# Keys ahead of queries, split projections stored in the layout of the tiles, and one product for the gates of all batches

## The chip, the cores and the metric

One core of a Trainium2 chip runs one program. The core has five engines with a queue of instructions each: TensorE (PE, matrix products; PEld is its loading of weights), VectorE (DVE), ScalarE (ACT), GpSimd (POOL) and SyncE (SP). SP issues most DMA transfers here, ACT and POOL a few. Each engine works through its queue in order and waits on semaphores where it needs another's result. The metric is the device time of one execution in microseconds. A time is the median of several runs; beside it there is one profiled execution, whose span and trace are quoted.

## The reference

A transformer block with adaptive layer norm, on 4 batches of 512 tokens of width 256, in float32:

```
mod = silu(c) @ wmod                      # six vectors of 256 for each batch: sa, ca, ga, sb, cb, gb
ga, gb: sign kept, magnitude at least 0.25
h = layernorm(x) * (1 + ca) + sa
x = x + ga * attention(h)                 # 32 heads of 8, 8 key/value heads, causal
h = layernorm(x) * (1 + cb) + sb
x = x + gb * ffn(h)                       # 16 experts of 176, 4 of them for each token,
                                          # and a shared expert of 352
```

The gate `ga` is needed where the attention is added to `x`, the vectors `sb`, `cb` and the gate `gb` only after that.

## The kernel before, in words

**Packs.** The attention is done in 16 packs, four for each batch. A pack has two key heads and their eight query heads. Queries and keys are split into three bfloat16 parts each (high, middle, low), so that one product of depth 72 (3 x 3 parts x 8) gives scores of float32 quality. For a pack, `qx` (a tile of 128 rows by 8 heads by 512 tokens) holds in its first 72 rows the query parts, and `kx` the key parts, arranged so that each pair of parts meets. There are three `qx` and three `kx`, used in turn by the packs.

**From projection to tile.** `norm1(b, due)` does a batch's first layer norm (`layernorm`: statistics, a power on POOL, four normalizations), two turns on PE with a modulating copy into `ht` on ACT, and then `split` for the queries of the first two packs, for the keys of all four packs, and for the queries of the last two; last `project_v` for the values. A `split` is a PE pass of two products, then on ACT and DVE in turn `high`, `rest`, `mid`, `low` into a tile `pt`, then stores from `pt` into small DRAM tensors on SP (line 762): `qd` (three parts by 64 rows by 512 tokens, 192 KB) and `kd` (48 KB) for each pack. `load(s)` (lines 815 to 822) reads them back into `qx` and `kx`: three transfers for the queries, each of 24 rows, and nine for the keys, each of 8 rows. For packs 0 and 1 ACT issues the key loads, for the others SP. Unused rows of `qx` and `kx` are filled once (`unused`, lines 512 and 513, on DVE; two of the three pairs wait for the first key store).

**Maxima, scores, weighing.** `row_max(s)` runs ahead of a pack: 22 units of PE products into two buffers `pr` (lines 860 and 868), each reduced to maxima on DVE (line 881). `shift(s)` splits the maxima in three parts (DVE), turns them (PE, line 920), copies them to `mrow` (ACT, line 930) and puts them as three more rows into `qx` with a transfer on SP (line 940, 24 KB). Only then can `pack(s)` compute scores (PE, line 1001), exponentials (ACT, 1013), the causal cut (POOL, 1020) and the weighing of values (PE, 971). `finish` copies the sum to `yr` (ACT, 1047), turns it and divides. After the fourth pack of a batch `after(b)` projects with `wo`, multiplies by the gate `g_sb` and adds to `x_sb`; `norm2(b)` does the second layer norm with `m2_sb`, the gating and the scattering of rows to the experts. The experts and the shared expert follow in `ffn`.

**Modulation.** `modulate_first` computes `sa` and `ca` for the first norm at the start. `modulation(b, last, due)` (lines 571 to 611), called for each batch in turn, computes the other four vectors: two PE passes of four products each (line 580), for which one batch's column of `sct` is repeated over 128 columns, so that the result stands in all 128 partitions. From the first pass `sign`, `size` and `gates` make the two gates (DVE, 128 x 512), from the second ACT copies the other two vectors into `m2_sb`.

**What sets the order.** The order on PE, DVE, ACT and SP is written out by a planner. `plan.add` takes an engine, an estimated cost, a function, the operations it needs, a due time (in packs), and what buffers (`hold`) it takes and gives. `plan.go` picks the operation that could start first by these costs, and among equals the one due first. The resulting order is fixed before the program runs; a wait that is longer than planned holds what is behind it on that engine. SP's transfers use eight semaphores in rotation, and a transfer waits until the one that had its semaphore before has landed.

**The start.** SP's order in the kernel before is: input loads with the first quarter of `x`; the stores and loads of packs 0 and 1; `later_loads` (line 1383: the other three quarters of `x`, and the weights of the gating, of the shared expert and of `wo`); the stores and loads of pack 2; `blank_all` (line 1394: 4.4 MB of zeros and one block of marked rows into DRAM); then the first `mrow` transfer. The calls of `modulation` wait for the loads of pack 1, and `norm1(1)` for `later_loads`.

## Time and profile before

| what | value |
|---|---|
| median of 3 runs | 754.57 us (753.82 to 755.66) |
| profiled execution: its time, its span | 746.31 us, 744.4 us |
| PE busy | 651.1 us (87%) |
| DVE busy | 455.6 us (61%) |
| share of the chain that ended last: PE, DVE, DMA | 66%, 17%, 6% |
| DMA packets | 54969, 74.51 MB |
| first product of the maxima, first of the scores | 31.0 us, 67.8 us |
| last `yr` copy of the attention | 421.9 us |

The profile page of one execution gives busy times of the engines, the span in 40 slices, the chain of work that ended last (followed back from the last instruction, at each step to what released it), the costliest groups of instructions, and the DMA issues. The trace can also be asked for the instructions of a stretch in order of time (start, duration, engine, source line, operation, output<-inputs; in brackets the idle time before it and what ended that), and for sums over stretches (busy time of each engine with its number of instructions, then the granted PE clock, the busy share of the 16 DMA engines, and what they moved). `SPq` and `ACTq` are transfers issued by SP and ACT: their duration is that of the issue, not of the transfer.

### The profile page before, as it was taken

How to read it: one execution, taken by the hardware profiler on the slowest of the kernel's cores; microseconds unless marked ns; L12 is line 12 of the kernel's file. 1: busy time of each engine (PE TensorE's matmuls, PEld its weight loads, DVE VectorE, ACT ScalarE, POOL GpSimd, SP SyncE). 2: the span in 40 equal slices, each digit the busy share in tenths (PEclk: the TensorE clock that was granted, in tenths of full speed). 3: DMA queues.
4: the chain of work that ended last, by engine and by line, in shares of the span. 5: the costliest groups of instructions: out<-in, count | busy, mean ns of one | idle time of the engine just before them, and what ended most of it. 6: DMA issues, size and time to landing. Idle time of an engine off the chain costs nothing.

```text
span 744.4 us, 12881 instructions
## 1 busy us (share of the span) xinstructions
PE 651.1 (87%) x4205; PEld 411.5 (55%) x4236; DVE 455.6 (61%) x1286; ACT 317.4 (43%) x557; POOL 346.2 (47%) x449
## 2 busy tenths in 40 slices
PE   5576999999999999999987897599999999999920
PEld 3343455555544554445443385488777777777710
DVE  4695868778888888787885056644333333333417
ACT  2103654575556654564655411022444444444400
POOL 4000222335257462673736643722566666556632
PEclk9787999999999999999999799799999999999965
DMA  4585211111133220332101196821576666666575
GB/s 135 128 253 198 72 27 41 42 42 47 29 100 102 65 64 13 108 102 57 42 11 55 63 300 200 205 69 30 96 110 110 109 110 110 102 108 110 66 188 186
DMA packets 54969, 74.51 MB, mean 100 GB/s; under 512 B 8024, under 2 KB 48056, under 8 KB 53752
## 3 DMA queue, kind: packets, MB, share of 16 engines
q1 hardware_dynamic: 37992, 51.99, 25.1%
q0 software_dynamic: 14448, 19.31, 16.0%
q10 hardware_dynamic: 2464, 2.39, 1.1%
q8 instruction: 35, 0.57, 0.3%
q14 instruction: 30, 0.25, 0.1%
HBM read 41.11 MB, written 32.16 MB: 98 GB/s over the span
## 4 chain that ended last, share of the span: by engine, by line
PE 66%; DVE 17%; DMA 6%; POOL 3%; issue 3%; ACT 2%; ACTq 0%; another core or an unknown queue 0%; SPq 0%; DVEq 0%; POOLq 0%
PE pu L1524 13%; PE py L1552 9%; PE pa L971 8%; PE pr L860 8%; PE p L1001 6%; DVE mx_s L881 6%; PE pu L416 5%; PE py L454 3%; PE pr L868 2%; PE pb L1543 2%; PE pt L1504 2%; DMA s<-acc_d 2%; PE p L580 1%; ACT ex L1013 1%; DMA kx<-kd 1%
## 5 line engine op out<-in xcount | busy, mean ns | idle before, releaser
L881 DVE TENSOR_REDUCE mx_s<-pr 128x1 f32<-128x384 f32 (+3 forms) x352 | 212.6, 635 | 52.6 <-PE pr L868 50.5
L1013 ACT ACTIVATE ex<-p 128x1024 f32<-128x1024 f32 (+1 forms) x192 | 163.2, 880 | 103.3 <-PE p L1001 77.4
L1020 POOL TENSOR_SCALAR_AFFINE_SELECT ex<-ex 128x256 f32<-128x256 f32 (+1 forms) x192 | 93.5, 493 | 180.2 <-ACT ex L1013 177.8
L1565 POOL DMA_INDIRECT acc_d<-y_b,token x79 | 123.0, 1556 | 77.2 <-DVE token L1514 32.3
L860 PE MATMUL pr<-kx,qx 125*128 125x384 bf16 (+3 forms) x512 | 125.2, 309 | 20.9 <-DVE mx_s L881 10.0
L1524 PE MATMUL pu<-up_sb,xt 128*128 x316 | 106.6, 460 | 0.0
L1001 PE MATMUL p<-qx,kx 128*128 128x384 bf16 (+3 forms) x481 | 92.0, 299 | 9.5 <-DMA qx<-mrow 6.5
L971 PE MATMUL pa<-ex,vaug 128*32 128x512 f32 (+3 forms) x1024 | 96.8, 450 | 2.5 <-POOL ex L1020 1.0
L860 PEld LDWEIGHTS <-qx 125*128 125x128 bf16 x512 | 47.0, 101 | 77.4 <-issue 49.7
L868 PE MATMUL pr<-seen,ident_h 128*128 128x128 bf16 (+2 forms) x352 | 88.5, 251 | 0.0
L1552 PE MATMUL py<-down_sb,at_b 88*128 x316 | 81.5, 379 | 1.2 <-DVE at_b L1547 1.2
L1342 POOL DMA_INDIRECT rows_d<-row,slot x64 | 64.2, 1003 | 25.7 <-DVE slot L1339 13.0
L1552 PEld LDWEIGHTS py<-down_sb,at_b 88*128 88x128 f32 x316 | 59.7, 189 | 21.9 <-ACT y_b L1562 1.7
L1538 DVE TENSOR_TENSOR a_b<-sg_b,pu 128x176 f32<-128x176 f32 x79 | 26.6, 337 | 71.7 <-ACT sg_b L1534 71.6
L1001 PEld LDWEIGHTS <-kx 128*128 128x128 bf16 x512 | 40.8, 98 | 40.9 <-issue 25.8
L1524 PEld LDWEIGHTS pu<-up_sb,xt 128*128 128x128 f32 x316 | 53.9, 190 | 16.7
L1562 ACT ACTIVATE y_b<-py,cw_b 128x256 f32<-128x256 f32 x79 | 37.4, 473 | 46.5 <-PE py L1552 46.5
L1547 DVE COPY at_b<-pb 88x256 f32<-88x256 f32 x79 | 33.2, 420 | 29.7 <-PE pb L1543 29.7
L1534 ACT ACTIVATE sg_b<-pu 128x176 f32<-128x176 f32 x79 | 25.1, 317 | 60.6 <-PE pu L1524 58.3
L416 PE MATMUL pu<-h2t,sup_sb 128*128 128x256 f32 (+1 forms) x192 | 48.2, 402 | 1.7 <-DVE a L436 1.7
L868 PEld LDWEIGHTS <-ident_h 128*128 128x128 bf16 x352 | 35.0, 99 | 22.8 <-issue 15.7
L416 PEld LDWEIGHTS pu<-h2t,sup_sb 128*128 128x128 f32 (+1 forms) x192 | 36.6, 193 | 9.8 <-DVE a L436 2.0
(176 smaller groups left out, 738.2 us busy)
## 6 DMA issues: line engine op xcount, KB each, us to landing
x<-rows_d SPq DMA_DIRECT2D x79, 136.5 KB
qx<-qd SPq DMA_DIRECT2D x48, 192.0 KB
up_sb<-in_up_t SPq DMA_DIRECT2D x8, 704.0 KB
acc_d<-blank SPq DMA_DIRECT2D x2, 2176.0 KB
qd<-pt SPq DMA_DIRECT2D x16, 192.0 KB
down_sb<-in_down_t SPq DMA_DIRECT2D x8, 352.0 KB
rows_d<-blank SPq DMA_DIRECT2D x17, 136.5 KB
x_sb<-in_x SPq DMA_DIRECT2D x4, 512.0 KB
```

The costliest lines, as they stand in the source:

```text
L416: nc.tensor.matmul(st["p"][:rows, w, :], lhsT=sup_sb[:, k, c0 : c0 + rows], rhs=h2t[:, k, c1 : c1 + half], start=(k == 0), stop=(k == KC - 1),
L860: nc.tensor.matmul(pr[:, h, :], lhsT=qx[s % 3][:QKZ, REP * j + r + h, ts(i, P)], rhs=kx[s % 3][:QKZ, j, :w], start=True, stop=False, skip_ ...
L868: nc.tensor.matmul(pr[:, :, w - P :], lhsT=ident_h, rhs=seen.unsqueeze(1).to_broadcast([P, n, P]), start=False, stop=True, skip_group_chec ...
L881: nc.vector.tensor_reduce(mx[s][:, i, c0 : c0 + n], st["pr"], AX.X, ALU.max)
L971: nc.tensor.matmul(st["pa"][32 * r : 32 * r + 32, c * P :], lhsT=vaugs[b % 2][:, c, SLOTS * n + j, :], rhs=exs[r], start=(j == 0 and c == ...
L1001: nc.tensor.matmul(pe[:, h, :], lhsT=kx[s % 3][:, j, ts(c, P)], rhs=qx[s % 3][:, REP * j + r + h, c * P :], start=True, stop=True,)
L1013: nc.scalar.activation(ex, st["pe"], AF.Exp, scale=qk_scale)
L1020: nc.gpsimd.affine_select(out=st["ex"][:, :, 0:P], in_=st["ex"][:, :, 0:P], pattern=[[0, n], [1, P]], base=0, channel_multiplier=-1, compa ...
L1342: dma = nc.gpsimd.indirect_dma_start(out=rows_d, out_offset=bass.IndirectOffsetOnAxis(ap=st["slot"][:, i, k : k + 1], axis=0), in_=st["row ...
L1524: nc.tensor.matmul(st["pu"], lhsT=st["xt"][:, k, :], rhs=up_sb[:, bass.ds(st["e"], 1), k, :].rearrange("p e f -> p (e f)"), start=(k == 0) ...
L1552: nc.tensor.matmul(st["py"], lhsT=st["at"][:, c, :], rhs=down_sb[:, bass.ds(st["e"], 1), c, :].rearrange("p e d -> p (e d)"), start=(c == ...
L1565: nc.gpsimd.indirect_dma_start(out=acc_d[j % 2], out_offset=bass.IndirectOffsetOnAxis(ap=st["token"][:, 0:1], axis=0), in_=st["y"], in_off ...
```

## The change

It has these parts.

1. `norm1` projects the keys first, then the queries of packs 0 and 1, then those of packs 2 and 3.
2. A pack's DRAM tensors `qd` and `kd` now have the 72 rows of the tile, so each part is stored three times (`store`: three transfers of 192 KB for queries, three of 48 KB for keys). `load` is then one transfer of 72 rows for the queries and one for the keys, in place of three and nine. `pt` has three buffers instead of two.
3. For batch 0 the stores are put in an order by hand (`stores`, `behind`): keys of pack 0, queries of pack 0, keys of pack 1, queries of pack 1, then the rest.
4. The second quarter of `x` is loaded with the inputs (`x_second`), and `norm1(1)` is called ahead of the maxima of packs 0 and 1. In the resulting order PE does the second batch's turns and its key projection ahead of the first maxima, and the query and value projections between them.
5. `modulation` for each batch becomes `modulations` for all: PE multiplies with the four columns of `sct` as they are, so the results stand in 4 partitions; the same DVE and ACT steps work on 4 x 512; the result goes to a DRAM tensor `m_d` of 16 KB, and two transfers spread it over all 128 partitions into `g_sb` and `m2_sb` (1 MB each). It waits for the `mrow` transfers of packs 0 and 1.
6. `later_loads` (now two quarters of `x` and the weights) waits for the `mrow` transfer of pack 1, `blank_all` for that of pack 3.

The resulting order on SP is: inputs; stores of packs 0 and 1; their query loads; stores of packs 2 and 3; loads of pack 2; 24 stores of the second batch; `mrow` of packs 0 and 1; loads of pack 3; the store and the two spreads of the modulation; `later_loads`; `mrow` of pack 2; loads of pack 4; `mrow` of pack 3; loads of pack 5; `blank_all`; `mrow` of pack 4; and so on. On ACT the key loads of packs 0 and 1 come after the first and the second copy into the second batch's `ht`. On DVE two of the fills of `qx` and `kx` come after the second batch's normalizations. The `mrow` transfer of pack 6 comes after the 24 stores of the third batch (before, after half of them). From pack 5 on the PE work of each pack is the same as before within a few units of maxima.

```diff
+            def load_x(b):
+                nc.sync.dma_start(
+                    out=x_sb[:, b * NT : (b + 1) * NT, :], in_=x_r[:, b * NT : (b + 1) * NT, :]
+                )
+
+            x_second = plan.add("SP", 0.5, lambda: load_x(1), due=-10.0, lag=12.0)
...
-            def modulation(b, last, due):
+            def modulations(last, stored, due):
 
                 st = {}
-                h1, h2 = hold("p1"), hold("p1")
+                m_d = dram.tile([B, 4, D], F32, name="mods", bufs=1)
+                op = last
+                mods = wts.tile([B, 4, D], F32, name="mods")
+                sign = wts.tile([B, 2, D], F32, name="sign")
 
                 def project(parts):
-                    st["p"] = ps1.tile([P, 2, D], F32, name="p1")
+                    st["p"] = ps1.tile([P, 2, D], F32, name="p1")[:B]
...
-                                lhsT=sct[:, k, b : b + 1].to_broadcast([P, P]),
+                                lhsT=sct[:, k, :],
...
+                def spread():
+                    nc.sync.dma_start(out=m_d, in_=mods)
+                    for t, at in ((g_sb, 0), (m2_sb, 2)):
+                        nc.sync.dma_start(
+                            out=t, in_=m_d[:, at : at + 2, :].unsqueeze(0).to_broadcast([P, B, 2, D])
+                        )
...
+                return plan.add("SP", 1.5, spread, [op, stored], due, lag=12.0)
...
-                first = [later, weighed.get(NPK * (b - 1) - 1)] if b else []
+                first = [later if b > 1 else x_second, weighed.get(NPK * (b - 1) - 1)] if b else []
...
+                    (wk_sb, NG * HD, kd, NPK * b, NPK, SLOTS),
                     (wq_sb[:, :, ts(0, P)], P, qd, NPK * b, n, PH),
-                    (wk_sb, NG * HD, kd, NPK * b, NPK, SLOTS),
                     (wq_sb[:, :, ts(1, P)], P, qd, NPK * b + n, n, PH),
...
                 def store(i, t):
-                    nc.sync.dma_start(
-                        out=t.rearrange("a p t -> p a t"),
-                        in_=st["pt"][i * rows : (i + 1) * rows],
-                    )
+
+                    parts = st["pt"][i * rows : (i + 1) * rows]
+                    order = "(n p d) h t -> n (d h) p t" if key[0] else "(p n d) h t -> n (d h) p t"
+                    for copy in t.rearrange(order, n=PT, p=PT):
+                        nc.sync.dma_start(out=copy, in_=parts)
...
+                if b > 0:
+                    stores(range(len(dst)), due)
+                elif not is_q:
+
+                    stores(range(1), due)
+                    behind.append(lambda q: stores(range(1, 2), due, q))
+                    behind.append(lambda q: stores(range(2, NPK), lambda: -0.6, stored[True, 1]))
+                elif behind:
+                    stores(range(1), due)
+                    behind[0](op)
+                    stores(range(1, 2), due)
+                    behind[1](op)
+                    behind.clear()
+                else:
+                    stores(range(len(dst)), lambda: -0.5, stored[True, 1])
...
+                def queries():
+                    nc.sync.dma_start(out=qx[s % 3][: PT * PT * HD], in_=qd[s])
+
+                def keys(queue):
+                    queue.dma_start(out=kx[s % 3][: PT * PT * HD], in_=kd[s])
...
-            later = plan.add("SP", 5.0, later_loads, [loaded[0][-1]], 0.0, lag=8.0)
-            plan.add("SP", 3.0, blank_all, [later, loaded[1][-1]], 1.0)
-            gates_made = loaded[1][-1]
-            due = Pace(0.5, 3.0, B * 6)
-            for b in range(B):
-                gates_made = modulation(b, gates_made, due)
+
+            norm1(1, Pace(-4.0, -1.6, 42))
             row_max(0)
             row_max(1)
+
+            gates_made = modulations(placed[0], placed[1], 1.5)
+            later = plan.add("SP", 4.0, later_loads, [placed[1]], 1.6, lag=8.0)
             for s in range(B * NPK):
                 b, n = divmod(s, NPK)
-                if n == 0 and b + 1 < B:
+                if n == 0 and 0 < b < B - 1:
                     norm1(b + 1, Pace(s - 0.5, s + 2.0, 42))
                 pack(s)
                 if s + 2 < B * NPK:
                     load(s + 2)
                     row_max(s + 2)
+                if s == 1:
+                    plan.add("SP", 3.0, blank_all, [placed[3]], 3.0)
```

## The prediction, made before the changed kernel was run

> **What bounds the kernel now.** I read the page first: spans, busy shares, the chain that ended last.
>
> ```profile
> span 744.4 us, 12881 instructions
> ...
> PE 651.1 (87%) x4205; PEld 411.5 (55%) x4236; DVE 455.6 (61%) x1286; ACT 317.4 (43%) x557; POOL 346.2 (47%) x449
> ...
> PE 66%; DVE 17%; DMA 6%; POOL 3%; issue 3%; ACT 2%; ACTq 0%; another core or an unknown queue 0%; SPq 0%; DVEq 0%; POOLq 0%
> ```
>
> PE carries the chain, so what shortens the whole is less PE work, or less time in which PE has none. The sums by stretch (cut at the first scores of the first pack and at the end of each pack, the `yr` copy) say where that is:
>
> ```profile
> core 0: us, PE busy (x) PEld busy (x) DVE busy (x) ACT busy (x) POOL busy (x), PEclk, DMA share, GB/s
> ...
> 20.00:31.00 11.00, 2.24 (x18) 1.95 (x17) 7.32 (x8) 2.25 (x5) 0.00 (x0) 0.78 0.54 122
> 31.00:53.30 22.30, 17.23 (x83) 11.04 (x84) 18.56 (x39) 0.66 (x2) 1.04 (x1) 0.81 0.77 218
> 53.30:67.80 14.50, 8.01 (x42) 4.24 (x40) 9.58 (x21) 3.41 (x4) 0.00 (x0) 0.74 0.94 315
> 67.80:90.30 22.50, 22.07 (x159) 9.98 (x162) 15.48 (x30) 13.91 (x19) 6.16 (x13) 0.94 0.19 45
> 90.30:116.00 25.70, 25.40 (x198) 14.21 (x199) 18.02 (x36) 13.45 (x20) 6.26 (x12) 1.00 0.16 41
> 116.00:139.20 23.20, 22.89 (x181) 12.95 (x183) 17.64 (x35) 12.58 (x18) 5.72 (x12) 1.00 0.13 34
> 139.20:157.80 18.60, 18.24 (x158) 8.88 (x159) 14.89 (x30) 11.37 (x15) 5.81 (x13) 1.00 0.17 43
> ```
>
> From 67.8 us PE is full and DVE is not; before it PE is far from full. From 31 to 53.3 DVE is the busiest (18.6 of 22.3). From 53.3 to 67.8 nothing is full but the DMA engines (0.94). The timeline and the chain, in order of time, name the transfer:
>
> ```profile
> 52.10 2.74 SPq L1396 DMA_DIRECT2D acc_d<-blank  x2
> ...
> 54.94 6.59 SPq L1400 DMA_DIRECT2D rows_d<-blank  x1
> ...
> 59.58 0.57 ACT L930 CAST mrow<-p 24x512 bf16<-24x512 f32 x1 [14.73 <-PE p L920]
> ...
> 61.62 1.06 SPq L940 DMA_DIRECT2D qx<-mrow  x1
> ...
> 67.76 0.59 PE L1001 MATMUL p<-qx,kx 128*128 128x512 bf16 x1 [4.95 <-DMA qx<-mrow]
> ```
>
> ```profile
> 21.44 1.79 DMA kd<-pt
> ...
> 27.62 3.06 DMA qx<-qd
> ...
> 61.62 6.10 DMA qx<-mrow
> ```
>
> Pack 0 cannot score until its row of maxima (24 KB) is in `qx`. That row was ready at 60.2, waited for SP, which was held by the blanks, and then took 6.10 us behind their 4.4 MB (343 GB/s, share 1.03, from 53 to 66).
>
> **The change, part by part.** The sum is made against the profiled execution (746.31 us, span 744.4), which lies 8.26 under the median of 754.57; I carry the difference over. Line numbers are those of the kernel before.
>
> *Second quarter of `x` early.* From 2 to 10 us the DMA engines move 307 GB/s and are then idle until the first store. 0.52 MB more takes 1.7 us, to about 11.7; DVE comes to it at 15.5, after the fills of `kx`, `qx`. Cost 0; without that cover every later DVE step slips by the lateness.
>
> *Keys first, stores tripled, loads merged.* Keys take the first projection's place (ends 16.75). DVE: keys' rest 17.4 to 18.1; ACT now does the queries' high part ahead of the keys' middle one (19.25 to 19.9); low part to 20.7. So the key store issues at 20.75, not 21.44. SP then issues 3 key stores of 0.35, 3 query stores of 0.60, and the same for pack 1: 5.7 us, and gaps. The query load of pack 0 issues at 26.8, against 23.17 to 27.62 for its three parts before. The last part took 3.06 us to land; three times the bytes (0.39 MB more at 343 GB/s, 1.15) make it 31.0. The key load stands on ACT behind the second batch's first `ht`: its four normalizations end on DVE at 23.8, turn and copy at 25.6, so it lands by 29 and is not last. PE's first maxima stand at 31.0, as before (31.02). DVE is ready at 30.9 too: the two other pairs of fills (3.05 each) now follow the second batch's normalization. Taken 0; ends −1 (keys alone count) and +3 (a whole landing more).
>
> [...]
>
> *Maxima of pack 0.* Before they ran from 32.07 to 53.3. DVE was busy 18.56, of it 6.9 other work (gates 3.6, statistics 2.5, normalizations 0.8). Now the other work is three splits, 6 x 0.69 = 4.1: 15.8. Three PE passes (two projections, one of values, 1.9 to 2.4 each at the low clock) stand between the maxima; DVE holds two buffers of them (1.3), so it waits about 1.1 each, and 1.4 elsewhere for PE's pace: 20.5 in all, end at 52.6. The gain is in what PE did meanwhile: the second batch's projections.
>
> *First scores.* Parts 1.07 (53.7), turn 0.6 (PE's order has two units of maxima ahead of it, not eight), copy 0.57: 55. SP has issued the second batch's last query store by 52.2 and is free. Landing: the key store was seen landed 1.81 after its issue; I take 2.1, so 57.1. PE's order also puts six more units of pack 1 first, paced by DVE from 53.7: scores at **57.7 instead of 67.76, −10.0**. Ends, those of the start included: −12 (DVE waits less) and −7 (low clock, row behind the last stores).
>
> *Work taken out of the full stretch.* After 67.76 the chain held, of the second batch, projections of 1.72, 1.86, 1.72 and 1.93, and five gate products of 1.74, 1.73, 1.78, 1.78 and 1.73: 16.0. Two products of 1.75 remain (same columns, whatever the rows): **−12.5**. That such passes count in full is seen from the packs: 25.7 less its 7.1 of passes is 18.6, 23.2 less 5.3 is 17.9, and a pack without any took 18.6. DVE's 7.4 (three of four rounds of 2.48) and ACT's 2.3 lie beside PE: 0.
>
> *Maxima deferred.* Before the first scores PE now does 8 units of pack 1, not 12; the order makes up for them only in pack 4. 4 x 0.55 (0.33 + 0.22): **+2.2**; ends 1 and 3.
>
> *Later transfers.* Pack 0 ends at 80.2, pack 1 at 98.8 (its 22.5 and 18.6). Load 3 waits for the last scores of pack 0 (before: issued 86.41, 3.9 ahead of the pack's end), so at 76.3. Behind it on SP stand the gates' store, their two spreads over 128 partitions (2.1 MB), the bulk loads (2.4 MB), and then pack 2's row of maxima. From 80.4 on 4.5 MB take 13.3 us at 338 GB/s (333 in the input loads of 36 to 46, 343 in the blanks): landed by 94. Pack 2 needs it 2.2 before pack 1's end (88.04 against 90.28 before), at 96.6. So **0**, with 2.6 to spare; at the rate per busy share of 84 to 92 (111 GB/s at 0.45, so 247) it is 18.2 us and +2.3. The trace has no spread from DRAM; I take the rate of the input loads, the nearest row, and keep 2.3. The blanks follow load 5 at 112.8 and end 15.5 later, before pack 4's row (needed at 133): 0.
>
> *Row of pack 6.* It now stands behind six query stores that wait for the third batch's last split. Before: parts done 201.3, split done 203.5, row issued 202.92, needed about 209.3. Now 203.5 + 6 x 0.6 + 2.1 = 209.4 plus gaps: **+1.0**; ends 0 and 4 (their 1.2 MB ahead of it). The other tripled stores lie in stretches where the DMA share is 0.13 to 0.32: 0, and the row's wait if that fills.
>
> Sum −10.0 −12.5 +2.2 +1.0 = **−19.3**: span 725.1, profiled 727.0, median **735.3**. From pack 5 on, PE's order has the same work as before, so the shift should reach the end.
>
> **Rivals.**
> 1. Rows of maxima late. They share SP with three times the store bytes and with the spreads. For it: the 6.10 us above. Against: the shares of 0.13 to 0.19 later. Spreads at half of 343 take 12.2, not 6.1: pack 2 loses 3.5; pack 6 loses 4: 7.5 in place of 1.0, **741.8**.
> 2. The start gains nothing: DVE paces the maxima, and the first scores stay near 67.8. For it: DVE 18.6 of 22.3. Against: 6.1 of the 14.5 after it is a landing. Only −12.5 stays: **742**.
> 3. More: the low clock (0.81, 0.74) lifts as PE idles less, and no row is late. First scores −14, deferred 1, row 0: −25.5, **729**.
> 4. Slower: the spreads read one 16 KB piece of DRAM from all engines at once and run far below any row here. Everything on SP's queue waits, pack 2's row first. Pack 2 may lose 19.3 before the gain is gone: 2.1 MB in 6.1 + 2.6 + 19.3 = 28 us, so below 75 GB/s, a third of the lowest rate above. At 60 GB/s (35 us) the loss is 26.3: **761.6**.
>
> **How the numbers follow.** Forecast 0.57, rivals 0.18, 0.05, 0.10 and 0.10. From 0.3% (2.3 us, what a measurement can tell from no change), of rival 4 0.02 ends within it: faster 0.90, same 0.02, slower 0.08. The forecast's own ends are −12, −12.5, +1, 0, 0 (low) and −7, −12.5, +3, +2.3, +4 (high): 731 to 744. The range 728 to 746 takes in rivals 1 and 2 and half of 3.
>
> **What would show it.** First scores near 57.7 with the row's landing about 2 us; PE's first maxima still near 31; two gate products, both after that; packs 0 to 3 ending near 80, 99, 117 and 135 (157.8 before, shift 22.5), then 20 after pack 4; no PE wait on `mrow` at packs 2, 4 above 1 us. Wrong if the spreads' window shows under 250 GB/s with PE waiting, if the first reduction comes after 35, or if a pack without passes takes over 20 us.

## The result, and the profile after

The changed kernel takes 753.14 us (median of 20 runs, 748.1 to 760.63) against 750.71 us before (20 runs, 744.52 to 755.66) on the same chip: ratio 1.0041, 95% interval 1.0017 to 1.0064. (Ratios here are estimated from the single runs and can differ by up to 0.2% from the quotient of the two medians, here 1.0032.) Where 19.3 us less was forecast, it is slower by 0.4%. The profiled execution took 751.28 us with a span of 749.5 (before 746.31 and 744.4). Its page:

```profile
span 749.5 us, 12663 instructions
...
PE 650.3 (87%) x4156; PEld 403.2 (54%) x4188; DVE 450.8 (60%) x1274; ACT 315.1 (42%) x551; POOL 346.0 (46%) x449
...
DMA packets 63392, 84.47 MB, mean 113 GB/s; under 512 B 7740, under 2 KB 55452, under 8 KB 62176
...
PE 64%; DVE 17%; DMA 8%; issue 3%; SPq 3%; ACT 2%; POOL 2%; another core or an unknown queue 0%; DVEq 0%; ACTq 0%; POOLq 0%
```

PE has 49 instructions less (48 from the one gate product), but is busy as long as before, and transfers (DMA and SPq) hold 11% of the chain that ended last, where they held 6%. The timeline of the start has the transfers and the work that waits for them:

```profile
29.26 3.27 SPq L853 DMA_DIRECT2D qx<-qd  x2
...
36.84 0.61 PE L890 MATMUL pr<-kx,qx 125*128 125x128 bf16 x4 [5.87 <-DMA qx<-qd]
...
45.25 8.31 SPq L785 DMA_DIRECT2D kd<-pt  x12
53.67 9.84 SPq L785 DMA_DIRECT2D qd<-pt  x12
59.44 0.57 ACT L960 CAST mrow<-p 24x512 bf16<-24x512 f32 x1 [5.37 <-PE p L950]
...
63.62 0.90 SPq L970 DMA_DIRECT2D qx<-mrow  x1
...
66.92 0.59 PE L1031 MATMUL p<-qx,kx 128*128 128x512 bf16 x1 [4.12 <-DMA qx<-mrow]
```

The first maxima start at 36.84 us, not 31.0. The row of maxima is ready at 60.0 but SP is still issuing the second batch's 24 stores, and sends it at 63.62; first scores at 66.92 instead of the forecast 57.7. Further on a row of maxima is late again, for pack 2 (PE has it 5.3 us after its issue, behind the spreads and the bulk loads) and for pack 6 (issued behind the third batch's stores):

```profile
89.49 0.24 SPq L613 DMA_DIRECT2D mods<-mods  x1
...
95.10 0.40 SPq L615 DMA_DIRECT2D g_sb<-mods  x1
...
106.47 0.75 SPq L970 DMA_DIRECT2D qx<-mrow  x1
...
111.78 0.38 PE L1031 MATMUL p<-qx,kx 128*128 128x512 bf16 x1 [1.75 <-DMA qx<-mrow]
...
183.03 18.64 SPq L785 DMA_DIRECT2D qd<-pt  x12
201.76 0.90 SPq L970 DMA_DIRECT2D qx<-mrow  x1
...
206.24 0.59 PE L1031 MATMUL p<-qx,kx 128*128 128x512 bf16 x1 [3.44 <-DMA qx<-mrow]
```

Before the change, the row of pack 6 went out ahead of the last stores, and PE did not wait for it:

```profile
202.34 0.56 ACT L930 CAST mrow<-p 24x512 bf16<-24x512 f32 x1
202.92 0.78 SPq L940 DMA_DIRECT2D qx<-mrow  x1
203.80 1.25 SPq L762 DMA_DIRECT2D qd<-pt  x2
```

The sums by stretch, for packs 0 to 3 and pack 5, and below them pack 5 before (columns: stretch, length, busy time and instructions of each engine, granted PE clock, DMA share, GB/s):

```profile
66.90:90.80 23.90, 23.50 (x167) 9.90 (x169) 15.43 (x30) 11.12 (x15) 5.75 (x12) 0.88 0.04 9
90.80:113.40 22.60, 20.07 (x166) 9.46 (x169) 16.82 (x33) 12.27 (x16) 5.84 (x12) 1.00 0.88 253
113.40:130.90 17.50, 17.05 (x154) 8.31 (x155) 13.99 (x29) 11.09 (x15) 6.10 (x13) 1.00 0.18 47
130.90:149.20 18.30, 17.90 (x157) 8.63 (x158) 14.64 (x31) 11.19 (x15) 5.69 (x12) 1.00 0.87 291
...
176.60:209.60 33.00, 26.95 (x219) 15.34 (x220) 24.84 (x79) 15.64 (x24) 11.78 (x21) 0.95 0.57 122
```

```profile
184.60:211.80 27.20, 25.38 (x215) 14.29 (x216) 24.36 (x77) 14.51 (x22) 9.48 (x19) 1.00 0.22 51
```

Pack 3 ends 8.6 us earlier than before (149.2 against 157.8). Pack 5 gives 5.8 back (33.0 against 27.2), packs 8 and 9 together 1.7 (55.9 against 54.2), packs 10 to 15 together 3.3 (121.4 against 118.1); packs 4, 6 and 7 take 0.8 less. The attention ends at 423.4 against 421.9.

### The profile page after: what moved, and what is told of

Its sections match the earlier page's. It is cut to its first block, busy times and chain, and to the rows that moved or that the text cites. A ratio compares the mean times of both kernels' runs of the same rounds, so it can differ in the third digit from the quotient of the medians.

```text
span 749.5 us, 12663 instructions
## 1 busy us (share of the span) xinstructions
PE 650.3 (87%) x4156; PEld 403.2 (54%) x4188; DVE 450.8 (60%) x1274; ACT 315.1 (42%) x551; POOL 346.0 (46%) x449
## 4 chain that ended last, share of the span: by engine, by line
PE 64%; DVE 17%; DMA 8%; issue 3%; SPq 3%; ACT 2%; POOL 2%; another core or an unknown queue 0%; DVEq 0%; ACTq 0%; POOLq 0%
PE pu L1553 12%; PE py L1581 9%; PE pa L1001 8%; PE pr L890 7%; PE p L1031 6%; DVE mx_s L911 5%; PE pu L416 5%; PE py L454 3%; PE pb L1572 2%; PE pt L1533 2%; SPq L785 2%; DMA qx<-mrow 2%; PE pr L898 2%; ACT ex L1043 2%; DMA x_sb<-in_x 1%
## 5 line engine op out<-in xcount | busy, mean ns | idle before, releaser
L1594 POOL DMA_INDIRECT acc_d<-y_b,token x79 | 123.1, 1559 | 77.0 <-DVE token L1543 56.5
L890 PE MATMUL pr<-kx,qx 125*128 125x384 bf16 (+3 forms) x512 | 123.6, 306 | 17.2 <-DVE mx_s L911 8.3
L1031 PE MATMUL p<-qx,kx 128*128 128x256 bf16 (+3 forms) x480 | 93.0, 301 | 14.2 <-DMA qx<-mrow 11.2
L1581 PEld LDWEIGHTS py<-down_sb,at_b 88*128 88x128 f32 x316 | 59.7, 189 | 21.9 <-ACT y_b L1591 1.7
L1031 PEld LDWEIGHTS <-kx 128*128 128x128 bf16 x512 | 41.4, 98 | 47.3 <-issue 32.5
```

What stands on the lines that cost most here:

```text
L890: nc.tensor.matmul(pr[:, h, :], lhsT=qx[s % 3][:QKZ, REP * j + r + h, ts(i, P)], rhs=kx[s % 3][:QKZ, j, :w], start=True, stop=False, skip_ ...
L1031: nc.tensor.matmul(pe[:, h, :], lhsT=kx[s % 3][:, j, ts(c, P)], rhs=qx[s % 3][:, REP * j + r + h, c * P :], start=True, stop=True,)
L1581: nc.tensor.matmul(st["py"], lhsT=st["at"][:, c, :], rhs=down_sb[:, bass.ds(st["e"], 1), c, :].rearrange("p e d -> p (e d)"), start=(c == ...
L1594: nc.gpsimd.indirect_dma_start(out=acc_d[j % 2], out_offset=bass.IndirectOffsetOnAxis(ap=st["token"][:, 0:1], axis=0), in_=st["y"], in_off ...
```

## The experiments

Three theories stood at the start. **A**: the tripled stores cost it, by their bytes and by SP's time. **B**: only the order on SP, where the rows of maxima stand behind something. **C**: the spreads, the late bulk loads and the early second norm. Ratios are to the kernel before on the same chip. One kernel run on two chips gave 0.9831 and 0.9883, so ratios from different chips are told apart only beyond about 0.5%.

**e1, single stores.** The changed kernel with the layout part undone: single stores, and loads of three and nine transfers again (`pt` keeps its three buffers).

```
-                    shape = [PT * PT * HD, rows, S]
-                    dst = [dram.tile(shape, BF16, name=name) for _ in range(n)]
+                    dst = [dram.tile([PT, HD * rows, S], BF16, name=name) for _ in range(n)]
...
-                    for copy in t.rearrange(order, n=PT, p=PT):
-                        nc.sync.dma_start(out=copy, in_=parts)
+                    nc.sync.dma_start(
+                        out=t.rearrange("a p t -> p a t"),
+                        in_=st["pt"][i * rows : (i + 1) * rows],
+                    )
...
```

> The changed kernel with its layout part undone: every part of queries and keys is stored once, and a pack is loaded with three transfers for the queries and nine for the keys, as before the change; all else stays. Three theories. A, store bytes: the tripled stores, at the 100 to 200 GB/s that the changed kernel's windows show for them, delay the first maxima (36.84 us against 31.02) and hold SP and the DMA engines when the rows of maxima of packs 0 and 6 should go out. B, SP's order alone: the rows stand behind other transfers on SP, and bytes do not matter. C, neither: the spreads of the gates, the late bulk loads and the early second norm cost what was gained. A: 739 us (736 to 743) on a scale on which the kernel before is 750.7 and the changed one 753.1; first products of the maxima at 31 to 32, first scores at 57 to 60, no wait of PE for the row of pack 6 above 1 us. B: 747, since SP issues 16 transfers fewer for a batch but the order stays; first scores near 63. C: above 750; first scores near 58 but the later packs as long as in the changed kernel.

Measured: 1.0112 (1.0077 to 1.0147), slower than the kernel before, and above the changed kernel's 1.0041. But the start came as forecast. In its timeline:

```profile
31.62 0.38 PE L895 MATMUL pr<-kx,qx 125*128 125x128 bf16 x4 [0.35 <-DMA kx<-kd]
...
56.54 0.63 PE L1036 MATMUL p<-qx,kx 128*128 128x512 bf16 x1
...
92.30 0.38 SPq L1425 DMA_DIRECT2D wo_sb<-in_wo  x1
93.79 0.32 SPq L852 DMA_DIRECT2D qx<-qd  x1
...
101.09 0.61 PE L895 MATMUL pr<-kx,qx 125*128 125x128 bf16 x4 [10.46 <-DMA qx<-qd]
...
146.53 0.59 PE L895 MATMUL pr<-kx,qx 125*128 125x128 bf16 x4 [6.80 <-DMA kx<-kd]
```

First maxima 31.62 and first scores 56.54, 10 us before the changed kernel. Then PE waits 10.5 and 6.8 us: with a load in three parts, each with its own due time, the planner put the last part of pack 3's load behind the bulk loads and that of pack 5 behind the blanks. The edit had brought its own fault; e5 mends it.

**e2, row on ACT.** The changed kernel with the row's transfer issued by ACT.

```
-                    "SP", 0.4, lambda: nc.sync.dma_start(out=qx[s % 3][QKZ:], in_=st["mrow"]),
+                    "ACT", 0.75, lambda: nc.scalar.dma_start(out=qx[s % 3][QKZ:], in_=st["mrow"]),
...
```

> The changed kernel with one thing moved: the transfer of a pack's row of maxima into qx is issued by ACT, right behind the copy that makes it, and so stands behind nothing on SP. A (store bytes at a slow rate): the issue comes 3.6 us earlier at pack 0 and about 4 at pack 6, but the first maxima stay at 36.8 and the landing is no shorter: first scores near 63.5, 747 us (745 to 750). B (SP's order): the rows of packs 0, 2 and 6 cost no PE wait above 0.5 us and the second half of the run is freed as well, 742 (739 to 745). C: 752 to 753.

Measured: 1.0028 (1.0004 to 1.0052), not told from the changed kernel. The first scores did move, to 62.76 from 66.92; packs 4 and 5 took 56.8 us (60.4 in the changed kernel, 54.0 before), packs 8 and 9 57.3 (55.9, 54.2). PE waits longer elsewhere: from 220 to 425 us its waits sum to 15.7 us, in the changed kernel to 11.8. Those that ACT ends have grown, for `ex` (2.0 against 1.0) and for `yr` (2.1 against 1.0); that the issues on ACT cause this is likely but not shown. Theory B in this form, a free queue for the row, falls.

**e3, the layout alone,** put into the kernel before (tripled stores, merged loads, third `pt`; the diff is that of e1 the other way round).

> The kernel before with the layout part alone: each part stored three times, one load of 72 rows for queries and one for keys, three buffers for pt. A: slower than before, first maxima 4 to 6 us later, and the row of pack 0 still behind the blanks: 756 us (753 to 760). B: about as before, 751, since the rows of maxima stand where they stood. C: as before, 750 to 752.

Measured: 1.0048 (1.0026 to 1.007). First maxima at 36.84, but all of it at the start: each pack from the second on ends 1.8 to 2.3 us later, none loses more. In its order pack 6's row (issued at 204.90) goes ahead of the last six query stores (205.78). So the tripling costs 0.5% here and more in the changed order.

**e4, gates and bulk loads,** put into the kernel before, without tripled stores, keys first and early norm.

```
...
+            gates_made = modulations(placed[0], placed[1], 1.5)
+            later = plan.add("SP", 4.0, later_loads, [placed[1]], 1.6, lag=8.0)
...
+                if s == 1:
+                    plan.add("SP", 3.0, blank_all, [placed[3]], 3.0)
```

> The kernel before with the other parts of the change except keys first and the early second norm: the second quarter of x early, one product for all gates with the spread through DRAM, the bulk loads behind the row of pack 1 and the blanks behind that of pack 3. No tripled stores. A and B: the row of pack 0 no longer lands behind the blanks (about 4 us less at the first scores), six gate products of 1.75 us fewer (10.5), less what pack 2's row loses behind the spreads (2 to 4): 740 us (737 to 744). C: the spreads and the late loads take it back, 749 or more, with PE waits on the rows of packs 2 to 4 of 8 us in all.

Measured: 1.0110 (1.0077 to 1.0142), with the same two waits as e1 (10.3 and 6.8 us), so again spoiled by late parts of loads; mended in e7.

**e5, single stores, one due time.** As e1, with

```
-                    due = s - 2 + b / PT
+                    due = s - 2 + (b / PT if s < 2 else -0.3)
```

> The run with single stores, with one thing more: the three query and three key transfers of a pack's load have one due time instead of three, so none of them is put behind the spreads, the bulk loads or the blanks on SP. In that run PE waited 10.5 us for the last query part of pack 3 and 6.8 us for keys of pack 5, and the clock was halved right behind both. Theory A (the tripled stores took the gain at the first scores; the late part of a load was a fault of the experiment's own order): the ratio to the kernel before falls from 1.011 by 17.3 us or more, to 0.980 (0.972 to 0.989), with pack 0 ending near 78.6, pack 1 near 98 and pack 3 near 135 us. Theory C (the spreads and the bulk and blank transfers in the full stretch take the gain whatever the stores do): the wait moves to the rows of maxima of packs 2 and 4, ratio 0.995 to 1.01. Theory D (PE at full load is slowed by the clock, so filled gaps come back as low clock): 0.995 to 1.005 without such waits, and more than 65 us of halved clock.

Measured: **0.9831 (0.9802 to 0.986)**, 738.43 us against 750.21. Theory A holds in size: undoing the layout makes the change a gain, and what separates this run from the changed kernel is the stores and loads of the layout. Whether their bytes cost, or the place of the rows behind them, it does not tell; e13 does. Packs 0 and 3 ended at 79.5 and 143.5 us. Pack 1 was still long, 24.5 us, with a PE wait of 3.2 us for the row of pack 2: part of C is true.

**e6, the same with the row on ACT** (the diff of e2 on e5).

> As the last run, with the transfer of the row of maxima issued by ACT. A: 1 to 3 us less than it, ratio 0.977, since the rows of packs 2 and 4 no longer queue behind bulk transfers on SP, though they share the DMA engines with them. C: the same as it within 1 us, since the engines and not SP's queue are what the row waits for. D: the same.

Measured: 0.9878 (0.9848 to 0.9909), beside e5 on the chip: no gain, rather 0.5% worse (the intervals overlap). Taking the row off SP's queue is not enough.

**e7, gates and bulk loads, one due time** (e4 with the line of e5).

> The kernel before with one product for all gates, the second quarter of x early, the bulk loads behind the row of pack 1 and the blanks behind that of pack 3, with the one due time for a pack's load. No tripled stores, queries first, the second norm where it was. Its first form lost 10.3 and 6.8 us to late loads and had ratio 1.011. A: 0.985 (0.977 to 0.992). C: 0.998 or more. D: 0.995 to 1.005 without waits for transfers.

Measured: 0.9896 (0.9865 to 0.9926); first scores at 60.77. The late bulk loads and the one product gain 1%; keys first and the early norm (e5 beside it) 0.65% more.

**e8, one product for the gates and its spreads alone;** bulk loads and blanks stay ahead of the first row.

```
...
-            for b in range(B):
-                gates_made = modulation(b, gates_made, due)
...
             row_max(0)
             row_max(1)
+            gates_made = modulations(placed[0], placed[1], 1.5)
```

> The kernel before with one product for all gates and its spreads alone (and the one due time); bulk loads and blanks stay ahead of the first row of maxima. A: six products of 1.75 us fewer, 10.5 us, less 0 to 2.3 for the spreads: ratio 0.988 (0.986 to 0.991), first scores still near 67. C: the spreads hold the row of pack 2, ratio 0.995 to 1.0. D: no gain, 0.997 to 1.003.

Measured: 0.9944 (0.992 to 0.9968), 4.2 us instead of 10.5. The first scores stand at 67.93, where they were, and PE waits longer ahead of them:

```profile
49.99 0.57 ACT L941 CAST mrow<-p 24x512 bf16<-24x512 f32 x1 [21.07 <-DMA kx<-kd]
52.35 2.77 SPq L1407 DMA_DIRECT2D acc_d<-blank  x2
55.21 6.52 SPq L1411 DMA_DIRECT2D rows_d<-blank  x1
61.83 1.07 SPq L951 DMA_DIRECT2D qx<-mrow  x1
...
67.93 1.01 PE L1012 MATMUL p<-qx,kx 128*128 128x512 bf16 x2 [14.44 <-DMA qx<-mrow]
```

The row is ready 11 us before SP sends it behind the blanks, and PE waits 14.4 us where it waited 5.0. The three gate products that were taken from this place had been free, since PE waits there anyway; only those behind the first scores count, five before and two now, which is 5.3 us.

**e9, tripled only from the second batch on.**

```
-                    shape = [PT * PT * HD, rows, S]
+                    shape = [PT * PT * HD, rows, S] if b else [PT, HD * rows, S]
...
+                    if b == 0:
+                        nc.sync.dma_start(out=t.rearrange("a p t -> p a t"), in_=parts)
+                        return
...
```

> Stores single in the first batch (packs 0 to 3, read in three and nine pieces with one due time) and tripled, with merged loads, in the other three batches; all else as in the changed kernel. It splits the 16 us that lie between the changed kernel (ratio 1.004) and the one with single stores throughout (0.983). Start alone: if the cost is the late first maxima, they come back to 32 to 33 us and the ratio is 0.983 to 0.987. Later batches alone: if the cost is SP held by the 24 stores of a batch when the rows of packs 0 and 6 are ready, the ratio stays at 1.000 to 1.005. Both, as I think: first maxima at 32, first scores at 61 to 63 instead of 57 since SP issues the second batch's 24 stores first, a PE wait of 2 to 4 us at pack 6 again: 0.994 (0.990 to 0.998).

Measured: 0.9992 (0.9963 to 1.0021): under the changed kernel by 0.5%, above e5 by 1.6%. First maxima 30.61, first scores 60.22 after a PE wait of 4.96 us for the row; waits of 2.9, 3.1 and 1.8 us for rows follow. Against e5, pack 0 ends 4.8 us later, pack 5 takes 3.7 and pack 9 4.1 us longer. By these ratios, which come from different chips, some three quarters of the cost lie in the later batches' stores, and the packs that grow are those whose row meets them.

**e10, tripled stores, merged loads cut in three.**

```
-                    nc.sync.dma_start(out=qx[s % 3][: PT * PT * HD], in_=qd[s])
+                    for b in range(PT):
+                        r = ts(b, PT * HD)
+                        nc.sync.dma_start(out=qx[s % 3][r], in_=qd[s][r])
...
```

> The changed kernel with its tripled stores kept but each merged load of 72 rows cut into three of 24 rows, for the queries and for the keys. If the first maxima come late because the stores issue and drain slowly (the load cannot start before 29 us and reads behind them): as the changed kernel, 1.004 (1.001 to 1.008), first maxima at 36 to 37.5. If the merged transfer itself is slow (210 GB/s over 72 rows): first maxima at 33 to 34 and the ratio 0.996 to 1.000.

Measured: 1.0080 (1.0051 to 1.0109), first maxima at 35.29. The first store went out earlier here, at 19.49 instead of 21.54; from there to the first maxima it is 15.8 us, in the changed kernel 15.3. So it is not the merged load, but what stands before it: 7.6 us for 12 stores on SP in both.

**e11, spreads and bulk loads behind pack 2's row,** on e5.

```
-            gates_made = modulations(placed[0], placed[1], 1.5)
-            later = plan.add("SP", 4.0, later_loads, [placed[1]], 1.6, lag=8.0)
...
+                    gates_made = modulations(placed[0], placed[2], 1.5)
+                    later = plan.add("SP", 4.0, later_loads, [placed[2]], 2.2, lag=8.0)
...
+                    plan.add("SP", 3.0, blank_all, [placed[4]], 4.0)
```

> Single stores with the one due time (ratio 0.983), and the gates' store and spreads and the bulk loads put behind the row of maxima of pack 2 instead of pack 1, the blanks behind that of pack 4. If the wait of 3.2 us for the row of pack 2, and the halved clock behind it, come from these transfers standing ahead of that row: both go, and the ratio is 0.977 (0.973 to 0.981). If the transfers cost the same wherever they stand in the full stretch: 0.982 to 0.986, with the wait at the load or the row of pack 4.

Measured: 0.9893 (0.9855 to 0.9931). Pack 1 fell to 20.6 us, pack 2 rose to 24.8 (19.4 in e5), with a PE wait of 4.1 us for the load of pack 4. The wait moved.

**e12, keys tripled, queries single,** on the changed kernel.

```
-                    shape = [PT * PT * HD, rows, S]
+                    shape = [PT, HD * rows, S] if out is qd else [PT * PT * HD, rows, S]
...
+                    if key[0]:
+                        nc.sync.dma_start(out=t.rearrange("a p t -> p a t"), in_=parts)
+                        return
...
```

> The changed kernel with the keys still stored three times and loaded with one transfer of 72 rows, but the queries stored once and loaded with three transfers of 24 rows. For a batch SP issues 16 stores instead of 24 (8 with single stores), but the bytes stored are 1.4 MB instead of 2.9 (1.0 with single stores). If the bytes and their slow rate are what costs: close to single stores throughout, 0.983 to 0.987, no PE wait for a row at packs 0 and 6 above 1.5 us, and first maxima before 33.5. If the number of transfers that SP issues ahead of a row costs: half of the 2.1%, 0.991 to 0.996, with first maxima near 34 and a wait of 2 us at packs 0 and 6. If it is below 0.983, the nine key loads of a pack cost SP something too, and this is the version to carry on with.

Measured: 0.9900 (0.9881 to 0.9919), on another chip than e5; first maxima 31.00, first scores 56.65. So at the start it is the tripling of the queries that costs, not that of the keys. Later PE waits 2.5 us for pack 10's row, and not at pack 6 (pack 5 takes 28.6 us). The ratio lies between the two readings and inside what chips differ by, so it decides nothing more.

**e13, the row ahead of the last stores.** All tripled stores stay; the last six query stores of a later batch wait for the row.

```
-                if b > 0:
+                if b > 0 and s0 == NPK * b + NPK // KC:
+                    late.append(lambda due, q: stores(range(len(dst)), lambda: due, q))
+                elif b > 0:
                     stores(range(len(dst)), due)
...
             row_max(0)
+            late.pop()(-0.5, placed[0])
...
                     row_max(s + 2)
+                    if late:
+                        late.pop()(s + 2.0, placed[s + 2])
```

> The changed kernel, tripled stores and all, with one thing moved: the last six query stores of the second, third and fourth batch go out on SP after the rows of maxima of packs 0, 6 and 10 instead of ahead of them. If what the tripled stores cost in the later batches is that these rows stand behind them (keys first put both query splits of a batch in front of the row; in the layout alone, with the old order of splits, the row of pack 6 went ahead of the last six): PE waits for rows fall to under 1.5 us at packs 0 and 6, pack 5 takes 28 to 29 us instead of 33, and the ratio falls from 1.004 to 0.992 (0.988 to 0.996), measured against the unchanged run of the changed kernel beside it about 9 us less. If the bytes alone cost, wherever they stand: within 2 us of it.

**e15, the changed kernel,** and **e16, single stores (e5), beside it.**

> The changed kernel as it is, beside the three others on one chip, since the comparisons so far were made on several. All theories: 1.004 (1.001 to 1.008).

> Single stores with the one due time, beside the changed kernel on one chip. If the tripled stores are the cause of what was missing: 0.983 (0.979 to 0.987), 2.1% under the changed kernel. If the earlier difference was one of chips: within 0.8% of it.

Measured on one chip: e13 **0.9901 (0.9879 to 0.9923)**, e15 1.0043 (1.0027 to 1.006), e16 0.9883 (0.9852 to 0.9914). One move of six stores gives 1.4% with every byte in place, nearly all that single stores give (1.6%). The timelines at pack 6, e15 first, then e13:

```profile
180.36 18.64 SPq L785 DMA_DIRECT2D qd<-pt  x12
194.58 0.57 ACT L960 CAST mrow<-p 24x512 bf16<-24x512 f32 x1 [1.10 <-PE p L950]
199.10 0.90 SPq L970 DMA_DIRECT2D qx<-mrow  x1
...
203.22 1.86 PE L1031 MATMUL p<-qx,kx 128*128 128x512 bf16 x4 [3.07 <-DMA qx<-mrow]
```

```profile
175.52 4.66 SPq L786 DMA_DIRECT2D qd<-pt  x6
189.30 0.56 ACT L963 CAST mrow<-p 24x512 bf16<-24x512 f32 x1
189.89 0.76 SPq L973 DMA_DIRECT2D qx<-mrow  x1
193.06 6.15 SPq L786 DMA_DIRECT2D qd<-pt  x6
```

In e15 the row is ready at 195.15 and waits 3.95 us for SP, which stands in a group of stores that itself waits for the batch's last split. In e13 it goes 0.03 us after it is ready, and PE does not wait. Pack 5: 28.8 against 32.9 us. At the start PE's wait for the row of pack 0 (3.07 us in e15 too) is gone as well: first scores at 62.29 against 64.97, though the first maxima come later (36.10 against 34.93). So what the tripled stores cost is mostly the order, theory B, although e2, which took the row to ACT, had gained nothing.

The late start itself weighs little here. In e16 the scores start 7.1 us earlier than in e13 (55.16), but pack 3 ends only 3.8 us earlier (137.9 against 141.7): PE then waits 2.8 us for the row of pack 2 (1.5 in e13) and 1.9 for that of pack 4. The medians differ by 1.1 us (736.01 against 737.15).

**e14, the same with single stores.**

> Single stores with the one due time, and the last two query stores of each later batch behind those rows of maxima. If rows behind stores are what costs: 0 to 3 us less than single stores alone, since only two stores move and PE waited under 1.5 us for those rows; ratio 0.980 to 0.983. If bytes: the same as it.

Measured: 0.9898 (0.9859 to 0.9936), no difference to e16: with two stores in the way instead of six, PE had not waited there.

**e17 and e18, the bulk loads at the start,** on e13 and on e14.

```
+            later = plan.add("SP", 4.0, later_loads, [x_second], -9.5, lag=12.0)
             norm1(0, Pace(-8.0, -4.0, 40))
...
-            later = plan.add("SP", 4.0, later_loads, [placed[1]], 1.6, lag=8.0)
```

> The changed kernel with tripled stores and the rows of packs 0, 6 and 10 ahead of the last query stores (ratio 0.990), and the bulk loads put right behind the second quarter of x, where the engines moved nothing from about 12 to 20 us. If the bulk loads in the stretch of pack 1 are what holds the row of pack 2: pack 1 takes 19 to 20 us instead of 22.4 and the ratio is 0.985 to 0.987; the first stores are not later. If the spreads (2.1 MB) alone fill that stretch, pack 1 stays at 22 and the ratio at 0.990.

> Single stores with those rows ahead of the last stores (ratio 0.990 beside 0.988 without), and the bulk loads at the start likewise. If the bulk loads hold the row of pack 2: pack 1 takes 19 to 20 us instead of 23.4, 0.983 to 0.985, which is near the 0.974 that was forecast for the change. If the spreads do: 0.988 to 0.990 as without.

Measured: **0.9826 (0.978 to 0.9873)** and **0.9807 (0.9764 to 0.985)**, 736.62 and 736.67 us against 751.15, both faster than the kernel before, and by these ratios than the changed one. Stretches of e17 (12 to 20 us, then pack 1), and pack 1 of e13:

```profile
12.00:20.00 8.00, 7.93 (x17) 3.17 (x17) 5.69 (x14) 2.88 (x5) 0.69 (x1) 1.00 0.91 284
83.70:104.30 20.60, 19.81 (x165) 9.40 (x167) 16.75 (x33) 12.20 (x15) 5.84 (x12) 1.00 0.53 154
```

```profile
83.50:105.90 22.40, 20.33 (x169) 9.47 (x168) 16.85 (x33) 12.29 (x16) 5.84 (x12) 1.00 0.88 254
```

The DMA engines carry the loads where they had moved next to nothing (3 GB/s from 12 to 20 us in the changed kernel), and pack 1 loses its wait: 20.6 against 22.4 us. The 20.6 are work: 165 products where the next pack has 154. The ratios come from another chip than those of e13 and e14, so that the bulk loads' share of the gain is shown only by pack 1.

## Why the prediction was wrong

**Keys first, stores tripled, loads merged (0, ends −1 and +3): +5.8.** This is the first step that failed. From the first store to the issue of the query load of pack 0 it took SP 7.7 us (7.6 of them for the twelve stores), not 6.1, and the load landed 7.6 us after its issue, not 4.2. The other 0.8 is that the first store went out at 21.54, not 20.75. (This start varies: in e15, the same kernel, the first store went out at 19.67 and the first maxima came at 34.93. From the one to the other it is 15.3 us in both, where 10.3 were forecast.) With single stores the first maxima stand at 30.4 to 32.6 (e1, e5, e16), so it is the stores; the merged load has no part in it (e10). The sum took of the stores only SP's issues, nothing for their bytes, and priced the load's extra bytes at 343 GB/s, read from the blanks. But the DMA engines were nearly full from 25 us until the load had landed: share 0.96 at 197 GB/s up to 29.3, then 0.88 at 214 up to 36.8. The trace of before had a store of queries at 185 GB/s (20.9 to 21.9 us), and it was not asked.

**Maxima of pack 0 (20.5): right.** From 37.91 to 57.89, 20.0.

**First scores (−10.0): −0.8.** "SP has issued the second batch's last query store by 52.2" was wrong by 11 us: 63.5. Of the 9.2 missing, 5.8 are the start's, 3.6 the row's wait for SP, and 1.2 its longer landing (3.3 against 2.1), less 1.4 elsewhere. With single stores the first scores came at 56.5, 57.3 and 55.2, against the forecast 57.7: the mechanism was right, but the time that it had to spare went to the tripled stores.

**Work taken out (−12.5) and deferred maxima (+2.2): right in kind.** Packs without a wait have the lengths that were forecast (17.5 and 18.3 for packs 2 and 3, against 23.2 and 18.6 before), and the product's part is seen in e8 (4.2 us where three products are 5.3). The deferred maxima are done in pack 1, not in pack 4 (166 products against 154 in pack 2, about 2 us).

**Later transfers (0, end +2.3): +4.0 in pack 1,** of which 2 are those maxima. The spreads waited 5.4 us for the gates' store; from 95.5 to 101 us the engines moved 206 GB/s, under the 250 that was named as a sign, and the row of pack 2 cost PE 1.75 us. Rival 4, far slower spreads, did not occur.

**Row of pack 6 (+1.0, ends 0 and 4): +5.8 in pack 5.** This is the second step that failed, and in the time the heavier one. The row did go out behind the six stores, as said. But they took 4.6 us (197.08 to 201.66), not 3.6, and PE had the row 4.5 us after its issue, not 2.1: a wait of 3.4 us, inside the ends. The clock was then halved from 205.6 to 209.0, and that was not priced. The row of pack 10 was taken at nothing with the other tripled stores. Rival 1, "Rows of maxima late", named the mechanism but put 6.5 us more on it; moving six stores of each later batch behind the rows of packs 0, 6 and 10 gives 10.6 (e13 against e15).

**From pack 5 on nothing changes: not so, and this is open.** Packs 10 to 15 took 121.4 us instead of 118.1; in e13 they took 120.8 and in e16 121.6, so it is not the tripled stores. After the attention the changed kernel needed 326.1 us, before 322.5, with the same 1302 products. But that compares one execution of each: e15, the same kernel, needed 324.4, and the profiled executions of all runs lie between 322.5 and 330.3. The granted clock differs (the last section); why was not settled.

So the loss came not from the one mechanism to which the prediction gave its chance of "slower" (the spreads) but from a term taken at zero and a wait priced at 1.0, both of the same stores. The best versions (e17, e18) reach 1.7 and 1.9% of the 2.6% that were forecast. The rest was not split further: e17 still has the late start, both have the longer packs 10 to 15, and one of them, e18, a wait of 1.5 us for the row of pack 4.

## What to carry to other kernels

One transfer in place of nine still waits for the stores that fill its source: before stores are tripled to save loads, read the rate of just these stores in the trace, and count the issues of the queue that they share with the one small transfer that everything waits for. Where a written order puts stores that wait for a late producer ahead of such a transfer, move the small one first; here that alone was worth 1.4%. An experiment that undoes a part gets its own order from the planner, so look at its waits before its ratio is believed (e1, e4).

## What the runs showed of the hardware

Transfers into DRAM were the slower, the fewer partitions they read. Three stretches of the changed kernel in which almost nothing else moves: key stores (16 partitions each), query stores (64) and blanks (128):

```profile
52.50:54.50 2.00, 1.57 (x15) 1.32 (x15) 1.35 (x4) 0.43 (x2) 0.00 (x0) 1.00 0.59 103
55.00:57.50 2.50, 1.80 (x12) 0.86 (x11) 2.50 (x5) 0.00 (x0) 0.00 (x0) 1.00 0.99 193
133.00:138.00 5.00, 4.97 (x41) 2.30 (x39) 4.61 (x9) 2.42 (x4) 1.26 (x3) 1.00 1.07 374
```

103, 193 and 374 GB/s. By the packets' records all three move their data in pieces of 1 KB, so the size of the pieces is not the reason. Over a longer stretch of query stores (55 to 63.5 us) it is 218. No run changed the number of partitions alone, so that it is the reason is not shown.

In the profiled executions before and after, the granted clock fell to a half for stretches of 3.4, 6.8 or 10.2 us, and at the end of each for over 30. In the changed kernel a product of the maxima over 512 columns (line 890) then took 0.63 us and the next one started 0.42 us behind it (at 207.90), at the full clock 0.38 and 0.22 (at 209.78). The clock was halved at a long wait of PE, from 205.6 to 209.0 at the wait for pack 6's row; in e1, behind the wait of 10.5 us, a product over 512 columns took 0.63 us too (line 903, at 101.49), later 0.38 (at 112.59). But it was also halved from 403.6 to 413.8 in the changed kernel, where PE's longest wait nearby was 1.5 us, so what sets it off is not shown. The wait of 3.4 us cost about 5, an estimate: the 2.8 us of work behind it, at half clock, are counted as 1.4 too long. Over all executions on one chip the mean granted clock was 0.947 before, 0.941 in the changed kernel (e15) and 0.946 in e13, where the waits for the rows behind the stores are gone. Over its whole span the execution profiled before was granted 0.946, that of the changed kernel 0.940, that of e15, the same kernel, 0.943 and that of e17 0.946. In the 63 us after the attention it was 0.86 before and 0.81 in the changed kernel and in e17:

```profile
421.90:485.00 63.10, 47.31 (x221) 38.74 (x222) 36.92 (x111) 8.54 (x20) 33.97 (x37) 0.86 0.75 218
```

```profile
423.40:486.50 63.10, 47.64 (x206) 37.97 (x206) 35.48 (x107) 7.76 (x18) 32.71 (x36) 0.81 0.74 215
```

Fewer products (206 against 221) in the same time of busy PE: about 3 us of the end of these two executions, by estimate (15 of 221 products that took 47.3 us).
